# Twenty shared 4 KB places in SBUF, and the second layer's first attentions issued during the first pass

## Chip, cores and metric

One core of a Trainium2 chip runs the kernel as one program. The metric is the device time of one execution in microseconds (us), lower is better. Engines are named as in the profile: PE (TensorE, matrix products), PEld (its weight loads), DVE (VectorE), ACT (ScalarE), POOL (GpSimd) and SP (SyncE, which here only issues DMAs).

## The reference, cut to what matters

Two layers run over `x` of shape (8, 512, 256) in float32, with a context of 64 tokens of 192 per batch. Each block is added to the residual stream and sees a normalized `x`.

```python
# layer 0: cross attention (8 heads of 64), then top-4 of 16 experts of size 64
x = x + _L0_xattn_ref(_layernorm(x), ctx_768, mask_BxS2_bk0, ...)
x = x + _L0_ffn_ref(_layernorm(x), ...)
# layer 1: this block, with 4 heads of 32 and top-32 of 64 keys per head
def _L1_xattn_ref(x_text, x_vision, ...):
    scores = einsum("bthd,bghd->bhtg", Q, K) / sqrt(DH)
    topv, topi = top_k(scores, 32)
    attn = zeros_like(scores).at[bi, hi, ti, topi].set(softmax(topv))
    c_t = einsum("btg,bgd->btd", attn.mean(axis=1), V)
    x = layernorm(x_text) * (1 + gate * scale_in(c_t)) + gate * shift_in(c_t)
    y = s4d(x, log_dt, A, C, D_skip)          # a long convolution over 512 tokens
    y = y * (1 + gate * scale_out(c_t)) + gate * shift_out(c_t)
    xt = x_text + y
    xt = xt + gelu(layernorm(xt) @ W1 + b1) @ W2 + b2
    return layernorm(xt)
x = x + _L1_xattn_ref(_layernorm(x), ...)
# layer 1: 8 experts, each takes the 512 tokens (of 4096) with its highest scores
x = x + _L1_ffn_ref(_layernorm(x), ...)
```

## The kernel before, in words

**Tiling.** The 4096 tokens are 8 batches of 512 (B, S), each four tiles of 128 tokens on the partitions (TPB). A batch of `x` is a tile of 128 x 1024 float32, that is 4 KB on each partition.

**Stages.** A *first pass* runs layer 0 for each batch b: `attend0(b)` (scores against `M0`, a softmax on DVE, POOL and ACT, values through `VO`), `route0(b)` (the gates; `wd` goes to DRAM and comes back spread over the partitions as `wB`), and `experts0(b)` (`xT` x `keys` into PSUM, then L754 on DVE turns the product into `wB`, then `wB` x `vals` on PE, and the result is stored to `mid_x`). Beside it, `conv_kernel` (`build`) makes the spectrum `Kf` of the long convolution in small DVE operations. A *second pass* runs most of layer 1: `attend1(b)` loads `xb` from `mid_x`, makes the scores (L902), runs the top-k of 32 in four rounds of MAX8 (L938) and MATCH_REPLACE (L939) per head and tile, then the weights (L919 to L928), transposes them and makes the filmed input `xi`; `convolve(b)` is the transform (`FX`), the product with `Kf` (L993, L1001) and the way back (`IW`), filmed again (`Fout`); `dense1(b)` is the two-layer GELU block (`hT`,`w` and `w`,`gT` matmuls); `settle(b)` and `offer(b)` normalize, score for the last experts and store `out` and `tab`. Then `ending` loads what the last experts need; a threshold search in 13 rounds finds each expert's 512 tokens; and the last stage runs the 8 experts (`listed`, `yT`, `fc1`, `gT`, `fc2`), gathering rows from `tab` and adding rows to `out` by indirect DMAs.

**What sets the order.** Both passes are Python generators, one per batch and stage, and each `yield` ends a step. A list `parts` (from L1212 on) holds (generator, number of steps, first due time, last due time); `emit` sorts all steps by due time and runs them in that order. A due time is in units of about one batch of the first pass and is written by hand. The tile framework then fixes each engine's instruction order and all waits before the run, from the order given, the dependencies and its own costs; on the chip each engine runs its list in order. `T2` = 7.967 is the due time at which the second pass starts, and batch b's second pass is shifted by `T2 + b`: its attention from `t + 0.047` to `t + 0.9`, its convolution to `t + 1.94`, `dense1` from `t + 2.25`. The experts of the first pass are due from b+1.6 to b+2.5.

**Where the data lie.** Tiles come from pools, and pools from two stacks, left and right. `M0` and `VO` (8 x 4 KB each), `xT`, the first pass's work tiles and those of `conv_kernel` lie on the left stack `sl`; `xa` (4 buffers), `keys`, `vals` and the routing's tiles on the right stack `sr`. `convolving` (due at T2) closes `sl` and only then allocates the pools of the second pass: `xb` (5 buffers), `xi` (3), the constants `wq1`, `mb1`, `tm`, `am`, the film weights, `FX`, and the work tiles of attention (`uT`, `qT`, `ex`, `sc1` with 5 buffers, `wrk1` with 4) and convolution (`t0` with 3, `t1` with 2). `dense` (due at 9.394) closes `sr` and allocates `IW`, `w1`, `w2` and the tiles of `dense1`, `settle` and `offer` (`hn`, `z`, `zT`). `ending` (due at T2 + 9.3) closes the second pass's left pools and allocates `fc_w` (two 8 KB buffers for each of the two weight matrices) for the last experts.

**Queues.** Nearly all loads and stores are issued by SP in program order: `xT`, `x`, `wd`, `wB`, `mid_x`, `xb`, `out`, `tab`, `fc`. A DMA that waits for its data or its buffer holds those behind it.

## Time and profile before

| | |
|---|---|
| time, median of 3 runs | 1293.17 us (1293.06 to 1298.84) |
| profiled execution, its own time | 1295.33 us |
| its span | 1293.6 us |
| mean granted PE clock | 0.942 |
| last matmul of the first pass (`wB` x `vals`) ends | about 505 us |
| first matmul of `dense1` (`hT` x `w`) | about 566 us |
| top-k (L938, L939) of batch 0, 1, 2, 3 runs in | 470 to 501, 518 to 553, 575 to 604, 633 to 664 us |
| threshold search | about 988 to 1016 us |
| matmuls of the last experts | 1036 to 1282 us |

How to read the profile: the page gives each engine's busy time over the span, then 40 slices of about 32 us in which a digit is the busy share in tenths (`PEclk` is the granted PE clock in tenths). A row of a stretch reads: from and to, length, then for each engine the busy us and the number of instructions, then the granted clock, the DMA share and GB/s. A row of a group reads: line, engine, operation, output and inputs, shapes, count, then busy us and mean ns, then idle time before it and what ended that. A row in order of time reads: start, length, engine, line, operation, and in brackets the idle time before it with what ended it. Matmuls are pipelined, so a matmul's recorded length is longer than its distance to the next one.

### The profile page before, as it was taken

What the parts mean: (1) busy time and instruction counts of PE and PEld (TensorE: products, weight loads), DVE (VectorE), ACT (ScalarE), POOL (GpSimd) and SP (SyncE); (2) the same over time, 40 slices, a digit from 0 to 9 for tenths busy, and PEclk for the clock granted to TensorE, in tenths of its full rate; (3) what the DMA queues carried; (4) which work ended last, traced back from release to release, by engine and by line L of the source; (5) the groups of instructions that cost most, each with busy time, mean ns of one, the idle gap of its engine ahead of it and who ended that gap; (6) DMA issues with size and microseconds to landing.
All of it is one profiled execution on the core that took longest, in us unless ns stands there. A gap on an engine that the chain in (4) does not pass through costs nothing. (4 is left out here: it accounts for less than half of the span.)

```text
span 1293.6 us, 16870 instructions
## 1 busy us (share of the span) xinstructions
PE 1140.8 (88%) x5468; PEld 719.7 (56%) x5468; DVE 791.0 (61%) x3334; ACT 395.9 (31%) x783; POOL 568.5 (44%) x800
## 2 busy tenths in 40 slices
PE   7998989888999979578899999998994299999995
PEld 3555656565666545245465565655673157666663
DVE  4479847748586468959799898988354602221110
ACT  2344121131313211032454555445343031222220
POOL 2333314323332212545678777777773114233331
PEclk9998999899999989789999999999997589999998
DMA  8003304303213423000010100000051014443321
GB/s 247 17 27 83 99 12 105 99 18 99 51 49 88 149 66 106 13 1 1 1 49 1 50 19 32 34 1 34 17 189 67 17 54 104 108 123 100 98 38 16
DMA packets 60749, 80.29 MB, mean 62 GB/s; under 512 B 6003, under 2 KB 45172, under 8 KB 60534
## 3 DMA queue, kind: packets, MB, share of 16 engines
q1 hardware_dynamic: 53254, 69.26, 18.0%
q0 software_dynamic: 6240, 8.79, 4.1%
q10 hardware_dynamic: 1168, 1.18, 0.3%
q8 instruction: 43, 0.70, 0.2%
q14 instruction: 44, 0.36, 0.1%
HBM read 62.04 MB, written 17.17 MB: 61 GB/s over the span
## 5 line engine op out<-in xcount | busy, mean ns | idle before, releaser
L259 PE MATMUL ps_o<-vals,wB 128*128 128x256 f32 x512 | 131.9, 404 | 21.5 <-DVE wB L754 21.4
L259 PEld LDWEIGHTS ps_o<-vals,wB 128*128 128x128 f32 x512 | 100.4, 202 | 54.7 <-DVE wB L754 29.9
L198 PE MATMUL ps_m<-hT,w 128*128 128x512 f32 (+1 forms) x288 | 125.3, 560 | 0.1
L259 PE MATMUL ps_o<-w,gT 128*128 128x256 f32 x512 | 122.6, 380 | 1.1 <-ACT gT L1055 1.1
L198 PE MATMUL ps_m<-xT,keys 128*128 128x512 f32 x256 | 122.8, 605 | 0.0
L1403 POOL DMA_INDIRECT out<-o,idx x32 | 52.0, 1626 | 154.7 <-DVE o L1402 89.7
L198 PE MATMUL ps_m<-yT,fc 128*128 128x512 f32 x256 | 116.9, 606 | 0.8 <-issue 0.8
L1401 DVE TENSOR_TENSOR o<-ps_o,bb 128x256 f32<-128x256 f32 x32 | 13.6, 425 | 166.1 <-PE ps_o L198 163.5
L198 PE MATMUL ps_o<-fc,gT 128*128 128x256 f32 x512 | 114.7, 379 | 0.1
L259 PEld LDWEIGHTS ps_o<-w,gT 128*128 128x128 f32 x512 | 95.4, 190 | 30.2 <-issue 14.9
L198 PEld LDWEIGHTS ps_o<-fc,gT 128*128 128x128 f32 x512 | 96.5, 190 | 19.7 <-issue 7.2
L656 POOL TENSOR_TENSOR sc<-sc,mx 128x512 f32<-128x512 f32 x32 | 34.3, 1079 | 123.5 <-DVE mx L655 73.6
L1396 ACT ACTIVATE gT<-ps_m,bb 128x512 f32<-128x512 f32 x64 | 44.0, 688 | 127.2 <-PE ps_m L198 127.2
L198 PEld LDWEIGHTS ps_m<-yT,fc 128*128 128x128 f32 x256 | 49.2, 195 | 54.2 <-issue 53.4
L939 DVE MATCH_REPLACE8 wrk<-top,wrk 128x64 f32<-128x64 f32 x384 | 78.0, 212 | 0.0
L754 DVE SCALAR_TENSOR_TENSOR wB<-ps_m,wB 128x512 f32<-128x512 f32 x64 | 43.1, 678 | 53.2 <-DMA wB<-wd 27.3
L1001 POOL TENSOR_TENSOR t<-t,t 128x768 f32<-128x768 f32 x32 | 58.4, 1847 | 38.6 <-DVE t L993 33.0
L198 PEld LDWEIGHTS ps_m<-hT,w 128*128 128x128 f32 x288 | 53.3, 194 | 37.4 <-issue 33.1
L1055 ACT ACTIVATE gT<-ps_m,b 128x512 f32<-128x512 f32 (+1 forms) x72 | 45.3, 634 | 85.4 <-PE ps_m L198 81.8
L198 PEld LDWEIGHTS ps_m<-xT,keys 128*128 128x128 f32 x256 | 48.5, 195 | 39.9 <-issue 36.0
L938 DVE MAX8 top<-wrk 128x8 f32<-128x64 f32 x384 | 65.6, 214 | 0.0
L198 PE MATMUL ps_m<-VO,eT 128*128 128x256 f32 x256 | 61.5, 383 | 3.9 <-ACT eT L670 2.6
(356 smaller groups left out, 2224.2 us busy)
## 6 DMA issues: line engine op xcount, KB each, us to landing
wB<-wd SPq DMA_DIRECT2D x64, 256.0 KB, 4.9
fc<-in_fc1T SPq DMA_DIRECT2D x8, 1024.0 KB, 4.9
fc<-in_fc2T SPq DMA_DIRECT2D x8, 1024.0 KB, 5.6
xT<-in_xT SPq DMA_DIRECT2D x8, 512.0 KB, 7.0
xa<-in_x SPq DMA_DIRECT2D x8, 512.0 KB, 7.9
mid_x<-xa SPq DMA_DIRECT2D x8, 512.0 KB, 3.0
xb<-mid_x SPq DMA_DIRECT2D x8, 512.0 KB, 5.6
tab<-zt SPq DMA_DIRECT2D x7, 528.0 KB, 3.0
```

What stands on the lines that cost most here:

```text
L198: nc.tensor.matmul(ps, lhsT, rhs, start=(i == 0), stop=(i == n - 1))
L259: nc.tensor.matmul(acc[j // 2][:, (j % 2) * D : (j % 2 + 1) * D], h[:, j * P : (j + 1) * P], rhs[:, f, :], start=(f == 0 and j % 2 == 0), ...
L656: nc.gpsimd.tensor_tensor(sc, sc, bcast(mx.unsqueeze(2), [P, H0, SC]), ALU.subtract)
L754: nc.vector.scalar_tensor_tensor(wB, ps, 0.0, wB, ALU.max, ALU.mult)
L938: nc.vector.max(m8, src[:, h, :])
L939: nc.vector.match_replace(wrk[:, h, :], m8, src[:, h, :], -FMAX)
L1001: nc.gpsimd.tensor_tensor(ts[0][:, i], ts[0][:, i], ts[1][:, i], op)
L1055: nc.scalar.activation(g, ps, AF.Gelu, bias=ns.b1[:, f : f + 1])
L1396: nc.scalar.activation(gT[:, f, :], ps, AF.Gelu_apprx_tanh, bias=ns.bb1[:, c : c + 1])
L1401: nc.vector.tensor_tensor(o, pso[:, :D], ns.bb2[:, e, :], ALU.add)
L1403: nc.gpsimd.indirect_dma_start(out=out, out_offset=bass.IndirectOffsetOnAxis(ap=idx[:, q : q + 1], axis=0), in_=o, in_offset=None, compute ...
```

## The change

One tile `places` of 20 x 4 KB per partition is allocated at the start and kept to the end, and a table says which tile lies in which place. `M0` and `VO` are views of places 0 to 15, `xa` takes 16 to 19, and the tiles of the second pass and of the last experts take the places of earlier users. What the second attention needs (`wq1`, `mb1`, `tm`, the two `am`, `qT`, `kblk`) is allocated at the start too, and a new part `for_second` prepares it. `film("in", b)` is called after the top-k instead of before it. `IW` is loaded in `convolving`. `k_t` in `conv_kernel` has half its size. The due times are new: `T2` is 6.886, the attentions of batches 0, 1 and 2 have due times of their own (5.5, 7.184, 8.7), and so have their convolutions (8.1, 8.66, 9.952).

```diff
+    am_of = [eb.tile([P, TPB, P], F32, name="am%d" % i) for i in range(2)]
...
+    aq = pool(ctx, "a1_q")
+    places = pool(ctx, "places").tile([P, 2 * B + TPB, TPB * D], F32, name="places")
+    PLACES = {
+        "xa": (16, 17, 18, 19),
+        "xb": (3, 10, 4, 11, 12, 19),
+        "xi": (13, 14, 15, 0),
+        "sc1": (1,),
+        "ex": (2,),
+        "uT": (8,),
+        "wrk1": (9,),
+        "hn": (16,),
+        "z": (17,),
+        "zT": (18,),
+        "Kt": (0,),
+        "yT": (3, 10),
+    }
+    def place(name, b):
+        own = PLACES[name]
+        return places[:, own[b % len(own)]].rearrange("p (j d) -> p j d", d=D)
...
-    xa = pool(sr, "xa", 4, side="right")
...
-        xs[b] = xa.tile([P, TPB, D], F32, name="xa")
+        xs[b] = place("xa", b)
...
-    M0 = cw.tile([P, 2, B, H0, SC], F32, name="M0")
-    VO = cw.tile([P, B, H0 // 2, D], F32, name="VO")
+    M0 = places[:, 0:B].rearrange("p b (k h j) -> p k b h j", k=2, h=H0)
+    VO = places[:, B : 2 * B].rearrange("p b (q d) -> p b q d", d=D)
...
+    m8 = load(aq, "mb1_u8", a["mask2"].partition_broadcast(P), [P, B * SC], U8, nc.scalar)
+    tm8 = load(aq, "tm8", a["tmask"], [P, NTILE], U8, nc.scalar)
...
+    def for_second():
+        nc.sync.dma_start(wq1, a["Wq1"].rearrange("(k p) n -> p k n", p=P))
+        yield
+        yield from centered(wq1, P, 1)
+        nc.vector.tensor_scalar(wq1, wq1, 1.0 / math.sqrt(32.0), None, ALU.mult)
+        nc.vector.tensor_scalar(mb1, m8, 1.0, FMAX, ALU.subtract, ALU.mult)
+        nc.vector.tensor_scalar(tm, tm8, 1.0 / H1, None, ALU.mult)
...
-                t = kts[0].tile([P, 2, nd, 16], F32, name="k_t")[:, :, :, :m]
+                t = kts[0].tile([P, nd, 16], F32, name="k_t")[:, :, :m]
                 tt(X[:, :, :, m : 2 * m], X[:, :, :, 0:m], zr, ALU.mult)
                 yield
-                for g in range(2):
-                    tt(t[:, g], X[:, 1 - g, :, 0:m], zi, ALU.mult)
+                for g, op in enumerate((ALU.subtract, ALU.add)):
+                    tt(t, X[:, 1 - g, :, 0:m], zi, ALU.mult)
                     yield
-                for g, op in enumerate((ALU.subtract, ALU.add)):
-                    tt(X[:, g, :, m : 2 * m], X[:, g, :, m : 2 * m], t[:, g], op)
+                    tt(X[:, g, :, m : 2 * m], X[:, g, :, m : 2 * m], t, op)
                     yield
...
-        ns.xb_p = pool(ctx, "xb", 5)
-        ns.xi_p = pool(ctx, "xi", 3)
...
+        ns.IW = load(a1c, "IW", a["IW"].rearrange("(f p) t -> p f t", p=P), [P, 4, P])
...
-        xb = xbs[b] = ns.xb_p.tile([P, TPB, D], F32, name="xb")
+        xb = xbs[b] = place("xb", b)
...
-            sc = ns.a1t.tile([P, H1, SC], F32, name="sc1", bufs=5)
+            sc = by_head(place("sc1", b))[:, j]
...
+        if b % 2 == 0:
+            film("in", b)
+        yield
         pa = ps_t(0)
...
-            ts = [ns.cvt.tile([P, 2, 3, D], F32, name="t%d" % c, bufs=3 - c) for c in range(2)]
+            ts = [
+                places[:, 5:8].rearrange("p s (n d) -> p (s n) d", d=D)[:, 6 * f : 6 * f + 6].rearrange(
+                    "p (u o) d -> p u o d", u=2
+                ),
+                ns.cvt.tile([P, 2, 3, D], F32, name="t1", bufs=2),
+            ]
...
-        f1 = ns.wpool.tile([P, 2, FF], F32, name="fc1")
+        f1 = places[:, 1:3] if e % 2 else places[:, 11:13]
...
-        f2 = ns.wpool.tile([P, NF, D], F32, name="fc2")
+        f2 = (places[:, 8:10] if e % 2 else places[:, 13:15]).rearrange("p s (c d) -> p (s c) d", d=D)
...
-    T2 = 7.967
+    T2 = 6.886
...
+        (for_second(), 3, 1.5, 3.0),
         (build, PARAM_STEPS, 1.17, 1.9),
-        (build, BUILD_STEPS - PARAM_STEPS, 1.9, 7.811),
+        (build, BUILD_STEPS - PARAM_STEPS, 1.9, 7.661),
...
-            (attend0(b), 10, b + 0.0, b + 1.0),
-            (route[b], 2, b + 1.0, b + 1.06),
-            (route[b], 2, b + 1.369, b + 1.555),
-            (experts0(b), 17, b + 1.6 + -0.05 * max(b - 5, 0), b + 2.5 + -0.05 * max(b - 5, 0)),
+            (attend0(b), 10, b + -0.111, b + 1.0),
+            (route[b], 2, b + 1.025, b + 1.04),
+            (route[b], 2, b + 1.135, b + 1.601),
+            (experts0(b), 17, b + 1.936 + -0.015 * max(b - 5, 0), b + 2.436 + -0.015 * max(b - 5, 0)),
...
-    parts += [(once(convolving), 1, T2, T2), (once(dense), 1, B + 1.394, B + 1.394)]
+    parts += [(once(convolving), 1, 8.01, 8.01), (once(dense), 1, B + 1.52, B + 1.52)]
+    early = (5.5, 7.184, 8.7)
     for b in range(B):
         t = T2 + b
+        u = early[b] if b < 3 else t
+        v = (8.1, 8.66, 9.952)[b] if b < 3 else t + 1
+        n = 0.5 if b < 3 else 1.0
         parts += [
-            (attends[b], 2, t + 0.047, t + 0.157),
-            (attends[b], 8, t + 0.145, t + 0.192),
-            (attends[b], 8, t + 0.192, t + 0.9),
...
-            (convs[b], 1, t + 1.071, t + 1.071),
-            (convs[b], 4, t + 1.2, t + 1.369),
...
+            (attends[b], 2, u + -0.02, u + 0.182),
+            (attends[b], 8, u + 0.249, u + 0.681),
+            (attends[b], 8, u + 0.681, u + 0.938),
...
+            (convs[b], 1, v + 0.035, v + 0.035),
+            (convs[b], 4, v + 0.224 * n, v + 0.5 * n),
...
-                (denses[b], 1, t + 2.25, t + 2.25),
-                (denses[b], 17, t + 2.28, t + 3.184),
-                (settle(b), 5, t + 3.131, t + 3.468),
...
+                (denses[b], 1, t + 2.7, t + 2.7),
+                (denses[b], 17, t + 2.718, t + 3.6),
+                (settle(b), 5, t + 3.628, t + 3.815),
...
-                u = t + 1.951 + 0.46 * h
+                u = t + 2.46 + 0.61 * h
...
-    parts.append((once(ending), 1, T2 + B + 1.3, T2 + B + 1.3))
+    parts.append((once(ending), 1, T2 + B + 1.946, T2 + B + 1.946))
...
-        yT = wk2.tile([P, 2, CAP], F32, name="yT")
+        yT = place("yT", e).rearrange("p (k j) d -> p k (j d)", k=2)
...
-        gT = wk2.tile([P, NF, CAP], F32, name="gT2")
+        gT = (places[:, 4:8] if e % 2 else places[:, 16:20]).rearrange("p s (f n) -> p (s f) n", n=CAP)
```

## The prediction

> **What bounds the kernel now.** I read the page first: busy shares, then the 40 slices.
>
> ```profile
> span 1293.6 us, 16870 instructions
> PE 1140.8 (88%) x5468; PEld 719.7 (56%) x5468; DVE 791.0 (61%) x3334; ACT 395.9 (31%) x783; POOL 568.5 (44%) x800
> ...
> PE   7998989888999979578899999998994299999995
> ...
> DVE  4479847748586468959799898988354602221110
> ...
> PEclk9998999899999989789999999999997589999998
> ```
>
> PE is the bound, but not everywhere: it sags in slices 14 to 19 (about 450 to 650 us) and in 30 and 31 (the threshold search), and the granted clock sags with it. DVE has slack in the first pass (283.6 of 425 us below) and stands mostly at 8 or 9 tenths from slice 15 to 27. So I took the busy time by stage, each cut where a first or last matmul of a kind stands: 505 us is the last matmul of the first pass (`vals`), 566 the first of `dense1` (`hT,w`), 985 about where the search begins.
>
> ```profile
> core 0: us, PE busy (x) PEld busy (x) DVE busy (x) ACT busy (x) POOL busy (x), PEclk, DMA share, GB/s
> 25.00:450.00 425.00, 392.60 (x2573) 250.09 (x2572) 283.60 (x824) 111.14 (x279) 139.33 (x217) 0.97 0.25 69
> 450.00:505.00 55.00, 46.20 (x157) 29.53 (x156) 41.35 (x258) 10.20 (x20) 10.21 (x21) 0.91 0.22 55
> 505.00:566.00 61.00, 38.84 (x93) 18.12 (x92) 49.62 (x267) 11.62 (x21) 34.50 (x47) 0.78 0.17 54
> 566.00:650.00 84.00, 74.86 (x241) 44.06 (x240) 65.36 (x378) 30.81 (x49) 43.18 (x56) 0.96 0.00 1
> 650.00:900.00 250.00, 236.08 (x907) 143.65 (x905) 228.69 (x1237) 125.77 (x230) 184.19 (x265) 1.00 0.09 29
> 900.00:985.00 85.00, 78.03 (x338) 54.33 (x337) 34.75 (x112) 39.28 (x86) 63.23 (x97) 0.95 0.28 94
> 985.00:1050.00 65.00, 27.52 (x137) 15.23 (x137) 33.24 (x144) 10.61 (x18) 12.50 (x18) 0.56 0.10 30
> ```
>
> The weak stretch is 505 to 566: 22 us of idle PE in 61, at a clock of 0.78. The order of time of PE there says why:
>
> ```profile
> 526.80 1.19 PE L198 MATMUL ps_m<-t,IW 128*128 128x256 f32 x2 [1.34 <-POOL t L1001]
> 529.61 2.05 PE L198 MATMUL ps_m<-F0Fout,amT 128*128 128x512 f32 x2 [1.62 <-DVE top L938]
> 533.26 2.93 PE L198 MATMUL ps_m<-t,IW 128*128 128x256 f32 x6 [1.60 <-POOL t L1001]
> 539.76 1.59 PE L198 MATMUL ps_m<-F0Fout,amT 128*128 128x512 f32 x2 [3.57 <-DVE top L938]
> ```
>
> The first pass is over, no `dense1` matmul is ready, and the convolution of batch 0 waits behind DVE's top-k (L938) of batch 1. This stretch is a matter of order; the work exists.
>
> **The change, term by term** (us, on the profiled span).
>
> *Gap between the passes.* In due times the last step of `experts0(7)` goes from 9.40 to 9.41 and the first step of `dense1(0)` from 10.217 to 9.586: the distance shrinks from 0.817 to 0.18 units. The 61 us of 505 to 566 make 75 us a unit there, so 0.18 is 13 us: **-48**. Ends: -38 (a gap of 23 us) to -61 (no gap).
>
> *What is moved in front.* The first attention of the second layer is now due at 5.5, 7.18 and 8.7 and the convolutions 0 and 1 at 8.1 and 8.66. So the PE work of 505 to 566 comes earlier (38.8 us busy at 0.78 of the clock, some 30 at full clock), and with it the attention of batch 2 and the convolution of batch 1, which ran after 566. I price these by the starts of matmuls in the order of time, 0.43 us apart for 512 columns, 0.215 for 256 and 0.11 for a transpose: attention 4 x 0.43 + 8 x 0.215 + 8 x 0.11 = 4.3, convolution 8 x 0.43 (`FX`) + 16 x 0.215 (`IW`) + 8 x 0.43 (`Fout`) = 10.3. Together 45 us, of which 12 stay in the remaining gap: 33 us are to be placed between 25 and 505. The cover is PE's idle time there, 32.4 + 8.8 = 41 us. At the share that the second pass reaches (236.08/250 = 0.944) 25 to 505 would take (392.6 + 46.2 + 33)/0.944 = 500 us instead of 480, +20; at the first pass's own share (0.924) 511, +31. I take **+25**; with no cover it is +33.
>
> DVE is the other cover. The costliest groups of one batch's attention there, over all eight batches:
>
> ```profile
> L939 DVE MATCH_REPLACE8 wrk<-top,wrk 128x64 f32<-128x64 f32 x384 | 78.0, 212 | 0.0
> L938 DVE MAX8 top<-wrk 128x8 f32<-128x64 f32 x384 | 65.6, 214 | 0.0
> ```
>
> and in the order of time on DVE:
>
> ```profile
> 480.93 0.60 DVE L938 MAX8 top<-wrk 128x8 f32<-128x64 f32 x4
> 481.44 0.07 DVE L939 MATCH_VALUE_LOAD wrk<-top,wrk 128x8 f32 x1
> 481.50 0.21 DVE L939 MATCH_REPLACE8 wrk<-top,wrk 128x64 f32<-128x64 f32 x1
> 481.63 0.08 DVE L939 MATCH_VALUE_LOAD wrk<-top,wrk 128x8 f32 x1
> ```
>
> The means of 0.21 us overlap: four MAX8 start within 0.51 us, and load and replace of one head are 0.127 apart from the next, so the 64 heads and rounds take 64 x 0.255 = 16 us. L902, L919, L921, L922 and L928 add (15.0 + 12.4 + 11.8 + 4.1 + 18.3)/8 = 8. That is 24 us a batch, and 72 for three; with some 36 for two convolutions' DVE part DVE would be at (283.6 + 41.4 + 108)/505 = 0.86 through the first pass, below the 0.91 (228.69/250) at which it runs beside a PE of 0.944. That the two mix is seen already: from 477 to 505 DVE was busy 27.3 of 28 us with this top-k, and PE 27.2 with `experts0(7)`. On POOL the attention is L941, L925, L924 and L883, (20.0 + 19.1 + 6.0 + 4.9)/8 = 6.3 us a batch, 19 for three, beside 139 busy of 425; on ACT its exponentials and copies are under 4 us a batch, beside 111 of 425.
>
> *The tail.* Six stretches of 54 us from 566 on hold one batch each; 900 to 985 holds the two batches with no attention beside them, 42.5 us each. With three attentions gone, batch 5 joins these: 54 - 42.5 = **-11**. Ends: 0 to -16 (the 14.6 us of PE work that left, at 0.92).
>
> *Experts later and denser.* `experts0(b)` moves from b+1.6..2.5 to b+1.936..2.436, its routing weights stay near b+1.1..1.6. The loads of `wB` so get a lead; DVE waited 27.3 us for them (L754, "DMA wB<-wd"), and PE 21.4 behind it, 13.9 of it between 25 and 450. That idle time is already spent as cover above, so 0, end -14. At the start `experts0(0)` is 0.34 units later, at some 55 us a unit up to +18 of idle PE if nothing else were ready; PE was busy 45.4 of 50 us between 75 and 125 with other ready work in its list. I take **+2**, nearer to the row that shows PE fed.
>
> *Shared places and DMAs.* Each place's earlier user is due well before the next one: `xb(0)` takes the place of `M0`'s batch 3, last read near 4.0, at 5.5; `t0` has two halves instead of three buffers, with 20 us and more between its users. `sc1` loses its fifth buffer: its L902 now waits for L941 on POOL (0.62 us) of the batch before, which ended some 20 us earlier in the windows of the second pass; behind it on DVE stands everything, `wB` included, so 0 with that cover and 0.6 us an event without it. `xb(5)` waits for the store of `xa(7)`, two units before; behind it on SP's queue stand only stores and later loads. Three loads of `xb` (512 KB, 5.6 us to landing), `wq1` and small rows move ahead on SP, past `wB` loads; the DMA share there is 0.25. `k_t` at half size makes L417's products alternate with their sums on one in-order engine, and the count stays. Two ACT queue loads come forward to the start. All this: **0**, end +5.
>
> *A rule that speaks against it.* The Trainium skill, "SBUF — State Buffer", section "Who interferes with whom": a DVE instruction with two SBUF inputs and a GpSimd instruction that reads SBUF exclude each other for the whole instruction. The trace does not show that price: POOL's 128x256 addition at L1040 has a median of 728 ns where DVE is 91% busy (566 to 900) and 726 where it is 41% (900 to 985). By the rule each of the 12 two-input L919 in three batches could hold POOL 0.42 us, an estimate of 5 us on an engine that is a third busy; by the row nothing.
>
> **Sum:** -48 + 25 - 11 + 2 = **-32**. The profiled execution took 1295.33 us around its span of 1293.6; the median shown is 1293.17. From the median: **1261 us**.
>
> **Rivals.**
>
> *No net gain.* The first pass grows by all that is put into it (+33), the gap stays at 23 us (-38), the tail gives nothing: -5, 1288, with 5 for DMAs 1293. For it: PE's idle pieces in the first pass are all under 4 us, so they take work in only if it is ready at that moment. Against: 477 to 505 us.
>
> *More.* The gap closes (-61), the work fits at 0.944 (+20), the tail gives 16: 1236. For it: `wB` in time, and no half clock between the passes. Against: PE never held 0.944 in the first pass.
>
> *Slower: DVE's order.* An experts step is 3.44 us of PE (two times 1.72 in the order of time) and one `wB` eviction of 0.68 on DVE, so DVE has 2.8 us to spare; a round of four heads is 1.02. Where three rounds stand ahead of an eviction, PE stalls. The attentions of batches 0 to 2 lie beside four batches' experts, 32 steps. An average stall of 1.0 us a step eats the gain; at 1.4 it is +45, **1306**. For it: PE's largest wait in the first pass is already this one (L259 on DVE wB). Against: the same 28 us.
>
> *It doesn't do what it says.* If the one tile of 20 places were tracked whole, every user would wait for every other, and the time would rise by hundreds of us. Against: `M0`, `scores` and `Kf` are single tiles used in parts, without such waits.
>
> **Chances.** Forecast (1240 to 1284) 0.60, more 0.10, none 0.13, slower by DVE's order 0.15, whole-tile waits 0.02. Within 0.5% (1286.7 to 1299.6) is about what a measurement of this kernel cannot tell from no change; I split "none" into 0.03 faster, 0.07 same, 0.03 slower. So faster 0.73, same 0.07, slower 0.20. The best ends give -48 + 20 - 16 - 14 = -58 (1235), the worst -38 + 33 + 18 = +13 (1306); 1237 to 1303 leaves out some 0.05 below and 0.12 above.
>
> **What would show it.** Right: top-k (L938) running before 450 us; the first `dense1` matmul less than 25 us after the last `vals` matmul; that last one at 525 to 540; the clock between the passes over 0.9; three batches at 43 us each before the search, which starts near 953. Wrong: last `vals` matmul after 560; PE waiting on DVE wB for over 50 us; a search at 985 or later; new waits that name places' users.

## The result: 6 us faster, and the profile after

The median fell from 1295.73 us (14 runs) to 1290.12 us (14 runs, 1286.31 to 1291.75): ratio 0.9954, 95% interval 0.9941 to 0.9967. Forecast were 1261 us and -32; the direction held, the size did not. The profiled execution has a span of 1286.4 us against 1293.6 before. First the page of after, the same lines as before:

```profile
span 1286.4 us, 16948 instructions
...
PE 1134.3 (88%) x5468; PEld 716.0 (56%) x5468; DVE 795.0 (62%) x3334; ACT 395.4 (31%) x781; POOL 568.4 (44%) x800
...
PE   7998989979899979998779999898974299999995
...
DVE  4459957847997884697987889795434602211110
...
PEclk9998989989899989999899999999997599999998
```

The sag of PE and of its clock between the passes is gone: slices 16 to 18 (counted from 0, 515 to 611 us) read 9, 9, 8, and the two digits 7 that follow (611 to 675 us) lie inside the second pass. Next the busy time by stage, cut at the same events: the last `vals` matmul is at 529 us (505 before), the first `hT,w` matmul of `dense1` at 542 (566 before), the search at 985 (991 before). The second fence is the kernel before from its first `dense1` matmul to its search, with the same columns.

```profile
core 0: us, PE busy (x) PEld busy (x) DVE busy (x) ACT busy (x) POOL busy (x), PEclk, DMA share, GB/s
25.00:450.00 425.00, 387.16 (x2546) 246.99 (x2547) 318.84 (x1144) 114.61 (x287) 143.49 (x225) 0.96 0.24 65
450.00:505.00 55.00, 48.52 (x177) 29.24 (x176) 38.30 (x151) 12.99 (x24) 16.19 (x22) 0.94 0.32 83
505.00:529.00 24.00, 24.00 (x89) 16.61 (x88) 10.97 (x29) 1.84 (x4) 6.30 (x5) 1.00 0.09 22
529.00:542.00 13.00, 10.97 (x32) 4.20 (x31) 10.42 (x23) 5.46 (x10) 8.93 (x15) 1.00 0.77 234
542.00:985.00 443.00, 394.18 (x1478) 241.10 (x1477) 330.10 (x1737) 197.05 (x366) 301.29 (x441) 0.97 0.11 35
```

```profile
566.00:991.00 425.00, 392.04 (x1495) 243.45 (x1494) 330.67 (x1733) 198.89 (x373) 294.66 (x426) 0.98 0.11 36
```

The gap of 61 us is 13 us at a clock of 1.00, as forecast. Up to the first `dense1` matmul the kernel is 24 us ahead. From there to the search it needs 443 us instead of 425 **for the same busy time** (PE 394.18 against 392.04, DVE 330.10 against 330.67), so 18 of the 24 us are lost there, 16 of them as idle time on PE. The lead shrinks at both ends of the stage. From the first `dense1` matmul to that of batch 2 the kernel after needs 136 us and the kernel before 123 (the same columns, after first):

```profile
542.00:678.00 136.00, 116.70 (x386) 67.44 (x385) 119.36 (x700) 50.20 (x83) 90.01 (x122) 0.95 0.03 7
```

```profile
566.00:689.00 123.00, 110.59 (x385) 66.16 (x384) 99.78 (x545) 51.80 (x87) 72.89 (x100) 0.97 0.05 14
```

PE is idle 19 us of this stretch instead of 12, while DVE does 20 us more: its top-k of batch 4 runs at 650 to 687 us, in front of the `dense1` of batch 2, and in the kernel before at 687 to 717. From there to the first `dense1` matmul of batch 6 both need the same (217 and 216 us), and from that one to the search 90 and 86 us. What follows the search takes some 302 us in both. The order of time on PE where the gap was (start, duration, what, in brackets the idle time before it and what ended it):

```profile
525.77 3.19 PE L259 MATMUL ps_o<-vals,wB 128*128 128x256 f32 x14
528.79 1.88 PE L198 MATMUL ps_m<-F0Fout,amT 128*128 128x512 f32 x4
530.87 1.96 PE L198 MATMUL ps_m<-F1Fin,amT 128*128 128x512 f32 x4 [0.20 <-DVE nm_a L161]
...
535.30 1.95 PE L198 MATMUL ps_m<-places,wq 128*128 128x512 f32 x4
...
541.60 0.66 PE L189 MATMUL ps_t<-ident,places 128*128 128x128 f32 x4 [1.41 <-ACT hT L1082]
542.09 1.88 PE L198 MATMUL ps_m<-hT,w 128*128 128x512 f32 x4
543.81 0.59 PE L198 MATMUL ps_m<-kblk,qT 128*128 128x256 f32 x2
```

The waits are at most 1.41 us. But `places,wq` at 535 and `kblk,qT` at 544 are the attention of batch 2: it was to be done by then, and it only begins. On DVE its top-k runs at 545 to 569 us; those of batches 0 and 1 at 322 to 357 and 424 to 460. In the kernel before they run at 469 to 499, 517 to 551 and, batch 2, 575 to 600. **At the first `dense1` matmul both kernels have two attentions behind them.** So the stage that follows holds the same work in both, as its busy time says.

### The profile page after: what moved, and what is told of

It is laid out like the page before. It is cut to its first block, busy times and chain, and to the rows that moved or that the text cites. A ratio compares the mean times of both kernels' runs of the same rounds, so it can differ in the third digit from the quotient of the medians.

```text
span 1286.4 us, 16948 instructions
## 1 busy us (share of the span) xinstructions
PE 1134.3 (88%) x5468; PEld 716.0 (56%) x5468; DVE 795.0 (62%) x3334; ACT 395.4 (31%) x781; POOL 568.4 (44%) x800
## 5 line engine op out<-in xcount | busy, mean ns | idle before, releaser
L259 PE MATMUL ps_o<-vals,wB 128*128 128x256 f32 x512 | 126.2, 391 | 10.8 <-DVE wB L801 10.7
L198 PE MATMUL ps_m<-places 128*128 128x512 f32 (+1 forms) x288 | 123.6, 604 | 0.7 <-ACT places L1430 0.7
L198 PE MATMUL ps_o<-places 128*128 128x256 f32 x512 | 114.7, 379 | 0.1
L198 PEld LDWEIGHTS ps_o<-places 128*128 128x128 f32 x512 | 96.5, 190 | 19.7 <-issue 7.2
L970 DVE MATCH_REPLACE8 places<-top,places 128x64 f32<-128x64 f32 x512 | 101.0, 203 | 0.0
L154 DVE BATCH_NORM_STATS2 bnst<-places 128x6 f32<-128x256 f32 x192 | 72.9, 414 | 20.9 <-POOL places L1117 12.8
L198 PEld LDWEIGHTS ps_m<-places 128*128 128x128 f32 (+1 forms) x288 | 51.4, 193 | 58.5 <-issue 52.6
L1441 ACT ACTIVATE places<-ps_m,bb 128x512 f32<-128x512 f32 x64 | 44.0, 687 | 126.7 <-PE ps_m L198 126.7
L969 DVE MAX8 top<-places 128x8 f32<-128x64 f32 x512 | 79.1, 206 | 0.1
L1040 POOL TENSOR_TENSOR places<-places,t 128x768 f32<-128x768 f32 x32 | 57.5, 1820 | 48.6 <-DVE t L1032 48.6
L189 PE MATMUL ps_t<-ident,places 128*128 128x128 f32 x256 | 49.0, 287 | 27.0 <-DVE places L720 7.9
```

The costliest lines, as they stand in the source:

```text
L154: nc.vector.bn_stats(st, src)
L189: nc.tensor.transpose(ps[:, j * P : (j + 1) * P], r[:, k * P : (k + 1) * P], ident)
L198: nc.tensor.matmul(ps, lhsT, rhs, start=(i == 0), stop=(i == n - 1))
L259: nc.tensor.matmul(acc[j // 2][:, (j % 2) * D : (j % 2 + 1) * D], h[:, j * P : (j + 1) * P], rhs[:, f, :], start=(f == 0 and j % 2 == 0), ...
L969: nc.vector.max(m8, src[:, h, :])
L970: nc.vector.match_replace(wrk[:, h, :], m8, src[:, h, :], -FMAX)
```

## The experiments

A table first, to read all of them by the same three cuts (us in the profiled execution): end of the first pass (last `vals` matmul), the gap from there to the first `dense1` matmul, the stage from that matmul to the search. The ratio is to the kernel before, timed on the same chip in turn, with its 95% interval.

| kernel | first pass ends | gap | stage | ratio |
|---|---|---|---|---|
| before | 505 | 61 | 425 | 1 |
| after | 529 | 13 | 443 | 0.9954 (0.9941 to 0.9967) |
| a_bnst8 | 533 | 14 | 451 | 1.0055 (1.0041 to 1.0069) |
| b_offers_later | 529 | 14 | 449 | 1.0011 (1.0000 to 1.0022) |
| c_attn2_early | 531 | 29 | 447 | 1.0121 (1.0106 to 1.0137) |
| d_before_bnst8 | 510 | 67 | 440 | 1.0152 (1.0138 to 1.0166) |
| e_places_old_due | 524 | 55 | 436 | 1.0180 (1.0166 to 1.0194) |
| f_none_early | 535 | 29 | 448 | 1.0159 (1.0145 to 1.0173) |
| g_conv2_first | 530 | 13 | 498 | 1.0389 (1.0364 to 1.0413) |
| h_before_shake | 507 | 60 | 424 | 1.0046 (1.0032 to 1.0060) |
| i_after_shake | 530 | 12 | 451 | 1.0055 (1.0037 to 1.0072) |
| j_no_move | 519 | 55 | 450 | 1.0246 (1.0230 to 1.0261) |
| k_dense_closer | 530 | 12 | 445 | 0.9978 (0.9969 to 0.9986) |
| l_before_first_dues | 506 | 70 | 427 | 1.0072 (1.0059 to 1.0085) |
| m_pad | 522 | 12 | 442 | 0.9892 (0.9875 to 0.9909) |
| n_no_move_pad | 509 | 54 | 453 | 1.0208 (1.0189 to 1.0226) |
| p_pad_dense_closer | 523 | 12 | 444 | 0.9925 (0.9908 to 0.9943) |
| r_before_slide | 517 | 60 | 424 | 1.0091 (1.0072 to 1.0111) |
| s_old_spacing | 522 | 13 | 464 | 1.0060 (1.0045 to 1.0076) |

### First theory: a queue cuts dense1(1)

In after, `dense1(1)` runs 20 of its 32 `hT,w` matmuls at 599 to 617 us and the other 12 only behind the matmuls of `offer(0)` at 659.7. Theory 1 said that this cut costs the time, theory 2 that too few attentions moved, theory 3 that the shared places make tiles wait. Four kernels:

```diff
 a_bnst8
-            st = small.tile([P, 6], F32, name="bnst")
+            st = small.tile([P, 6], F32, name="bnst", bufs=8)
 b_offers_later (both lines; batch 6 keeps its time)
-                (offers[b], 1, t + 4.1 - 0.25 * (b == B - 2), t + 4.1 - 0.25 * (b == B - 2)),
+                (offers[b], 1, t + 4.5 - 0.65 * (b == B - 2), t + 4.5 - 0.65 * (b == B - 2)),
 c_attn2_early
-    early = (5.5, 7.184, 8.7)
+    early = (5.5, 7.184, 7.95)
 e_places_old_due (and every other due time of the kernel before)
-    T2 = 6.886
+    T2 = 7.967
```

> The changed kernel with eight buffers instead of four for the small tile bnst (the statistics of one row tile, L153), nothing else. Theory 1 (queues): in the changed kernel the additions of dense1(0) are done on DVE at 577.9 to 579.1 us, but its mv_out aggregates run only at 641.9 to 643 us, because the four bnst buffers are handed out in program order and conv(2)'s statistics stand ahead while conv(2) itself waits behind the top-k of batch 3; so settle(0) and offer(0) come late, and dense1(1), of whose 32 hT,w matmuls 20 run at 599 to 617 us, stops until offer(0)'s matmuls at 659.7 us. With eight buffers the aggregates come before 620 us, dense1(1) loses less than 15 us in the middle, and the time falls by 10 to 18 us, to 1272 to 1280. Theory 2 (DVE as a whole bounds the second pass, because only two of eight attentions moved): the statistics move, but the time does not: within 4 us of the changed kernel. Theory 3 (waits on the shared places): within 4 us too, and dense1(1) still stops.

> The changed kernel with the due times of offer(0) to offer(5) 0.4 of a batch later (4.5 and 4.579 instead of 4.1 and 4.179), so that all of dense1(b+1) stands ahead of offer(b) on PE and in the two buffers of ps_m(1). Theory 1 (queues): dense1(1) is no longer cut at step 5 of 8: its 32 hT,w matmuls run without the stop from 617 to 660 us, the batch of dense work that is left over after the last offers gets 12 matmuls shorter (about 11 us of PE's time), and the kernel gets 6 to 12 us faster, to 1278 to 1284. Theory 2 (DVE bounds the second pass): the order on PE changes, the time does not, within 4 us. Theory 3: within 4 us.

> The changed kernel with the second attention of batch 2 due at 7.95 instead of 8.7, and nothing else. Its top-k runs at 545 to 569 us in the changed kernel, after the first pass, while those of batches 0 and 1 run at 322 to 357 and 424 to 459 us. Theory 2 (too little moved): the top-k of batch 2 comes before 530 us, DVE, which is busy 10 to 12 of 25 us from 475 to 525 us, takes it there for nothing, the second pass has 24 us of DVE less, and the kernel gets 8 to 15 us faster, to 1275 to 1282. Theory 1 (queues): the cut of dense1(1) stays, because it hangs on conv(2) and the statistics behind it; 0 to 5 us faster. Theory 3: 0.

> The storage of the changed kernel (twenty shared places, the constants of the second attention loaded early) with all due times of the kernel before: no second attention stands beside the first pass. Theories 1 and 2: the places cost nothing by themselves, so the time is that of the kernel before within 5 us (against the changed kernel: 2 to 10 us slower). Theory 3 (the shared places make tiles wait for one another): over 6 us slower than the kernel before, with waits of the loads into xa or xb or of the first writes of ex, wrk1, z and zT for the last reader of another tile.

None came out as theory 1 or 2 had it. b does what it says: the 32 matmuls run through, to 629 us. But `dense1(2)` starts at 678 us, as in after. Four stretches of 25 us show what became of the gap on PE, first of after, then of b (columns as above):

```profile
625.00:650.00 25.00, 16.86 (x44) 8.43 (x45) 19.12 (x71) 8.94 (x17) 16.56 (x29) 0.82 0.00 0
650.00:675.00 25.00, 21.23 (x86) 12.36 (x85) 25.00 (x167) 10.90 (x22) 22.14 (x27) 0.97 0.01 1
```

```profile
625.00:650.00 25.00, 21.48 (x73) 12.10 (x72) 19.00 (x64) 10.34 (x21) 15.78 (x27) 0.93 0.00 0
650.00:675.00 25.00, 15.20 (x53) 6.81 (x53) 25.00 (x157) 7.99 (x19) 22.70 (x29) 0.81 0.00 1
```

PE's hole moved from the first stretch to the second; DVE is busy 19 and 25 of 25 us in both kernels. Theory 1 falls: work that PE does earlier there is missing later. a still had the cut (`dense1(1)` to 672 us), so it tests less than it was meant to. In c the top-k of batch 2 did come early, at 490 to 529 us, and the stage from the first `dense1` matmul to the search did lose DVE work:

```profile
560.00:1007.00 447.00, 394.25 (x1457) 241.56 (x1456) 306.79 (x1520) 192.38 (x361) 287.92 (x420) 0.95 0.11 35
```

306.79 against 330.10 us of DVE, about the 24 us of one attention, and yet 447 us of stage; and with that top-k among the convolution of batch 0 on DVE (its products at 509 to 527, its `yv` at 534 to 543) the first `dense1` matmul went from 542 to 560. So theory 2 has no support either: in this order, with a third attention out of the stage, nothing is won. e was 24 us slower than before; the waits in it that name the earlier user of a place are small (loads of `xb` behind a store of the place, 5.1 us in two of them, on SP's queue alone). The storage seemed to cost 24 us, unless old due times on new storage are bad for another reason; further down 5 to 12 us of it are found, and the rest of e's 24 stays open.

### How much an edit without meaning costs

All engines' orders are made anew from every edit. So two kernels got an edit that changes no work: more buffers for `bnst` in the kernel before, and one due time shifted by 0.02 in both.

```diff
 d_before_bnst8
-            st = small.tile([P, 6], F32, name="bnst")
+            st = small.tile([P, 6], F32, name="bnst", bufs=8)
 h_before_shake, i_after_shake
-        (build, PARAM_STEPS, 1.17, 1.9),
+        (build, PARAM_STEPS, 1.17, 1.88),
```

> The kernel before with eight buffers instead of four for the small tile bnst, nothing else: the control of a_bnst8. The first four runs overturned theory 1 (the cut of dense1(1) went away in b_offers_later and the kernel got 5 us slower) and showed that three edits of the changed kernel that each do what they say (a_bnst8, b_offers_later, c_attn2_early) lose 5 to 20 us. Theory 4 (order): the orders of all five engines are made anew by every edit, the due times of a kernel were fitted to its own orders, and an edit that is worth nothing by itself loses some 5 to 20 us. Then this one, whose two orders differ in the same way, is 5 to 20 us slower than the kernel before. If instead the number of buffers had a cost or a gain of its own in the changed kernel alone, this one is within 4 us of the kernel before.

> The kernel before, in which the last of the first filter parameters are due at 1.88 instead of 1.9 of a batch, an edit that changes no work and no storage: a shake of the order. Theory 4 (order): 5 to 20 us slower than the kernel before, and the ends of the value matmuls of the eight batches move by several us against 144, 192, 241, 301, 356, 404, 461 and 505 us. Theory 3 (the shared places cost 24 us by themselves, as e_places_old_due would have it): the order is robust, within 4 us of the kernel before.

> The changed kernel with the last of the first filter parameters due at 1.88 instead of 1.9: the same shake that made the kernel before 5 us slower (h_before_shake), no work and no storage changed. Theory 4 (order): 0 to 20 us slower than the changed kernel's 1290. If the order is robust in the changed kernel: within 4 us.

The ratio moved by +1.52%, +0.46% and, against after, +1.01%: 6 to 20 us. The net result of the change, 6 us, is no larger than the smallest of these, so how much of it the change earns and how much this order is not shown. From here on I read totals only for effects above this and otherwise the end of a stage: the first pass is steadier, it ends at 505, 510, 507 and 506 us in the four kernels with the old storage and no move (before, d, h and l, which comes below), and at 529, 529, 530 and 533 in after, b, i and a. The stage behind it is not steady: the shakes alone move it from 425 to 440 (d) and from 443 to 451 (i).

### The move taken back

```diff
 f_none_early
-    early = (5.5, 7.184, 8.7)
+    early = (T2, T2 + 1, T2 + 2)
-        v = (8.1, 8.66, 9.952)[b] if b < 3 else t + 1
+        v = (8.1, 8.9, 9.952)[b] if b < 3 else t + 1
 j_no_move (early as in f, and)
+    T2 = 7.967
+        v = t + 1
+        n = 1.0
```

> The changed kernel with the second attentions of batches 0, 1 and 2 due as those of the others are, at 6.886, 7.886 and 8.886 instead of 5.5, 7.184 and 8.7 (conv(1) at 8.9 instead of 8.66, since it follows its attention); storage and all other due times stay. It takes back the move of the attentions alone. If the move is worth what the prediction gave it (48 us of gap less 25 us of work in front): the top-k of batch 0 comes after 420 us, that of batch 1 after 500 us, the first pass ends 10 to 20 us earlier than at 529 us, the gap in front of the first dense1 matmul grows from 13 to 40 us or more, and the kernel gets 15 to 30 us slower than the changed one, 1305 to 1320. If the gain of the changed kernel came from its other due times: within 8 us of the changed kernel.

> The changed kernel with the second pass due 1.081 of a batch later (T2 = 7.967 as in the kernel before) and no attention earlier than that: storage, the due times of the first pass and the spacing inside the second pass stay. The move itself is taken back whole. By the prediction's terms (gap of 48 us come back, 25 us of work in front gone, 11 us of tail gone, the other way round): the first pass ends at 505 to 515 us, the first dense1 matmul comes at 560 to 575 us, and the kernel is 25 to 40 us slower than the changed one, 1315 to 1330, that is slower than the kernel before, because the other due times were set for the move. If the move is worth little: within 10 us of 1290.

f takes back less than it was meant to: with T2 still 1.08 units earlier, the top-k of batch 0 runs from 387 us and that of batch 1 from 469, both still in the first pass, which ends at 535 us and not 10 to 20 us earlier than in after; the gap is 29 us, not 40. It loses 2% against after. j takes back all: the gap is 55 us again, the kernel 2.9% slower than after (1.0246 against 0.9954), 37 us, and slower than the kernel before, as expected. **With the rest of the change kept, the move is worth 37 us here and 41 us between n and m below**, more than any shake above and about the -34 of the three terms that the forecast had for it (-48, +25, -11). The rest of the change, without the move, costs 32 us against the kernel before; part of that can be the order, since no due time was fitted to this kernel. One thing did not fit: the first pass of j, with no more beside it than in the kernel before, ends at 519 us, not at 505 to 510.

### What lengthens the first pass: a slide

```diff
 l_before_first_dues (route, build and dense in the same way)
-            (attend0(b), 10, b + 0.0, b + 1.0),
+            (attend0(b), 10, b + -0.111, b + 1.0),
-            (experts0(b), 17, b + 1.6 + -0.05 * max(b - 5, 0), b + 2.5 + -0.05 * max(b - 5, 0)),
+            (experts0(b), 17, b + 1.936 + -0.015 * max(b - 5, 0), b + 2.436 + -0.015 * max(b - 5, 0)),
```

> The kernel before with the changed kernel's due times for the first pass alone (attend0, route, experts0, the filters' end at 7.661, dense at 9.52); storage and second pass stay. The first pass of the changed kernel ends 24 us later than before, but its first three batches, beside which no second attention ran, are late already by 5, 9 and 9 us. If the work moved in front sets the end of the first pass (the prediction): this one ends the first pass at 505 us give or take 5. If the due times of the first pass do: 512 to 520 us. The time of the whole lies 0 to 20 us above the kernel before by theory 4.

The first pass of l ends at 506 us: its due times are not it. So it is the storage (e: 524, j: 519). The DMA issues on SP's queue show a difference in every kernel with the places. Here, in order of time, a line of PE and a line of SP's queue of the kernel before, and then the same two of after:

```profile
71.83 1.25 PE L198 MATMUL ps_m<-wo,vT 64*64 64x256 f32 x10
```

```profile
73.15 1.20 SPq L448 DMA_DIRECT2D ldt<-in_log_dt  x2
```

```profile
84.59 1.98 PE L198 MATMUL ps_m<-ctxT,wv 96*128 96x512 f32 x4
```

```profile
86.66 1.20 SPq L496 DMA_DIRECT2D ldt<-in_log_dt  x2
```

Each load starts within 0.1 us of the end of a matmul that reads weights: before, the last `wo,vT` (71.83 + 1.25 = 73.08); after, the last `ctxT,wv` (84.59 + 1.98 = 86.57).

`ldt` and its neighbours are the parameters of the filter that `build` makes. After takes `Kt` (4 KB) and `dskip` (1 KB) out of the pool `kg`. The pool `kp` of the parameters lies behind it and slid down by 5 KB, as these two lines say from memory last read by the `wo,vT` matmuls onto memory last read by `ctxT,wv`, 13 us later. So the filter starts 13 us later, and its DVE work falls more into the time from 100 us on, where `wB` is due. To test it, 5 KB were put back in front of `kp` in three kernels, and in r the slide was made alone in the kernel before:

```diff
 m_pad (on after), n_no_move_pad (on j), p_pad_dense_closer (on k)
             with ExitStack() as sp:
+                pool(sp, "pad").tile([P, TPB * D + D], F32, name="pad")
                 yield from params_in(pool(sp, "kp"))
 r_before_slide (on the kernel before)
-        dskip = kg.tile([1, D], F32, name="dskip")
-        Kt = kg.tile([P, TPB, D], F32, name="Kt")
...
                 yield from seeds(pool(sp, "ks"))
+            kl = pool(stack, "kl")
+            dskip[0] = kl.tile([1, D], F32, name="dskip")
+            Kts[0] = kl.tile([P, TPB, D], F32, name="Kt")
```

> The changed kernel with an unused tile of 5 KB in front of the filter's parameter tiles (pool kp), which puts these back on the memory that they have in the kernel before; it is given back before the next pool opens. In all six kernels with the shared places so far that were looked at, the load of ldt is issued at 85.6 to 86.7 us, right behind the last ctxT,wv matmul, and in the four with the old storage at 73.2 to 74.7, right behind the last wo,vT matmul: with Kt (4 KB) and dskip (1 KB) taken out of the pool below, the parameter tiles slid onto weights that are still read. Theory 6 (slide): ldt is issued at 73 to 78 us, PE's waits for wB between 100 and 210 us fall, the second batch ends its value matmuls at 192 to 196 us instead of 201, the first pass ends 5 to 12 us before 529 us, and the kernel gets 3 to 12 us faster, to 1278 to 1287. Theory 4 (order): ldt comes early, but the time is not below the changed kernel's by more than 3 us.

> j_no_move (storage of the changed kernel, no attention moved) with the same 5 KB in front of the parameter tiles. j_no_move ends its first pass at 519 us, the kernels with the old storage at 505 to 510. Theory 6 (slide): 506 to 513 us, and 5 to 15 us faster than j_no_move's 1327. If other parts of the storage lengthen the first pass: still 516 us or later.

> The kernel before with Kt and dskip allocated behind the parameter tiles instead of in front of them: the slide alone, with the old storage. Theory 6: ldt is issued at 84 to 88 us instead of 73, the second batch ends its value matmuls 5 to 9 us after 192 us, the first pass ends at 510 to 520 us instead of 505, and the kernel is 5 to 25 us slower than before (the shake of the order, 5 and 19 us in h_before_shake and d_before_bnst8, is in it). If the late parameters cost nothing: the first pass ends within 3 us of 505 to 510 us.

m_pad loads `ldt` where the kernel before does (SP's queue in order of time):

```profile
73.26 1.20 SPq L497 DMA_DIRECT2D ldt<-in_log_dt  x2
```

and what PE waits for `wB` between 100 and 210 us (in total, times, longest) is, in the waits of before, of after and of m_pad in turn,

```profile
PE ps_o L259 <- DVE wB L754: 5.1, 6, 1.7
```

```profile
PE ps_o L259 <- DVE wB L801: 8.6, 3, 4.2
```

```profile
PE ps_o L259 <- DVE wB L802: 2.5, 1, 2.5
```

The second batch ends its value matmuls at 193 us (before 192, after 201), the first pass at 522 instead of 529, and in n at 509 instead of 519. r, with the slide alone, loads `ldt` at 86.4 us and ends the first pass at 517 instead of 505. In four pairs the ratio moves the same way: after to m -0.62%, j to n -0.38%, k to p -0.53%, before to r +0.91%, that is 5 to 12 us. Each alone is no more than a shake of the order, and the second batch is not a sure sign: r ends it at 196 us, short of the 5 to 9 us that were expected, and a, e and i, which load `ldt` late too, at 193 to 195. The third batch is: in the eight kernels of the table that load `ldt` at 73 to 75 us it ends its value matmuls at 241 to 245 us, and PE waits 2.5 to 6.0 us for `wB` between 100 and 210; in the eleven that load it at 86 to 87 us, at 249 to 255, with 7.5 to 12.0 us of waits. With that, and four pairs of one sign, the slide is shown. **m_pad is the fastest kernel of the study: 1279.3 us, 1.1% under the kernel before.**

### The second pass: not settled

```diff
 k_dense_closer (s in place of t for dense1, settle, offer and the tail)
+        s = t - 0.21 * min(b, 2)
 g_conv2_first
-        v = (8.1, 8.66, 9.952)[b] if b < 3 else t + 1
+        v = (8.1, 8.66, 9.7)[b] if b < 3 else t + 1
 s_old_spacing (on m_pad; all other due times of the second pass as before, but for batches 0 to 2)
-    T2 = 6.886
+    T2 = 7.336
```

> The changed kernel with dense1, settle and offer due 0.21 of a batch earlier for batch 1 and 0.42 earlier for batches 2 to 7, the spacing behind the attention that the kernel before has. In the changed kernel dense1(5) starts 99 us behind the end of the top-k of batch 5, in the kernel before 79 us; dense1(5) to dense1(6) takes 53 us although all top-k is done at 856. Theory 5 (the dense work was put half a batch further behind the attention, so what three early attentions gained is given back at the end): the distance falls to 75 to 85 us, the search begins before 975 us and the kernel is 10 to 20 us faster than the changed one, 1270 to 1280. Theory 4 (order): the distance falls, but holes appear elsewhere on PE; not faster by more than 4 us.

> The two edits of the changed kernel together that have a reason in the traces: the 5 KB in front of the parameter tiles and dense1, settle and offer closer behind the attention (k_dense_closer, 1291). If theory 6 holds and the order does not eat it: 1278 to 1287. By theory 4: 1288 to 1305.

> The changed kernel with the convolution of batch 2 due at 9.7 instead of 9.952, in front of the top-k of batch 3 on DVE instead of behind it. In the changed kernel DVE runs that top-k at 598 to 626 us, yv of conv(2) only at 627 to 640, PE waits for it (4.3 us at 628) and has 12.0 and 18.6 us of work in the two 25 us stretches from 625 to 675, and dense1(2) starts at 678 us. Theory 2a (top-k(3) in front of conv(2) makes the hole in PE's work): dense1(2) starts before 665 us, and the kernel is 5 to 15 us faster than the changed one. Theory 4 (order): dense1(2) starts earlier too, but the top-k of batches 3 to 7 come later by as much and the kernel is within 5 us of the changed one or slower.

> m_pad with the spacing of the kernel before inside the second pass (attention and convolution of batches 3 to 7, dense1, settle, offer and the tail, T2 = 7.336 so that dense1(0) stays due at 9.6); the three early attentions stay as they are. From the first dense1 matmul to the search the five profiled kernels with the old spacing take 424 to 440 us (425 in the kernel before), the kernels with the new one and no move 450 to 453, and with the move 442 to 447. Theory 7 (the move does save the forecast 7 to 11 us there, but the new spacing costs 17 to 25): about 415 to 430 us here, the search begins at 950 to 965 us instead of 976, and the kernel is 10 to 25 us faster than m_pad, 1254 to 1270. Theory 4 (order: the old spacing is only good with the old order): 440 us or more, not faster than m_pad.

k did bring `dense1(5)` from 99 to 80 us behind the top-k of its batch, and the stage stayed at 445 us; with the pad (p against m) it is 0.3% slower. g put the convolution first as meant, and PE's in-order queue stopped elsewhere: the transposes of `offer(0)` waited for POOL's part of `settle(0)`, and `dense1(1)` behind them. PE's waits in g have this line:

```profile
PE ps_t L189 <- POOL places L1117: 17.3, 2, 16.5
```

s was to bring the stage to 415 to 430 us and needed 464. Its stretches, columns as above:

```profile
600.00:625.00 25.00, 23.84 (x84) 15.41 (x83) 9.37 (x24) 6.08 (x11) 11.42 (x13) 1.00 0.01 2
625.00:650.00 25.00, 11.35 (x40) 4.65 (x38) 25.00 (x196) 13.63 (x27) 19.98 (x32) 0.66 0.00 0
675.00:700.00 25.00, 24.28 (x101) 15.37 (x100) 15.28 (x93) 8.30 (x17) 8.71 (x10) 1.00 0.15 43
700.00:725.00 25.00, 13.35 (x24) 6.68 (x24) 24.62 (x144) 2.99 (x5) 13.37 (x20) 0.59 0.06 22
```

PE runs through three batches of `dense1` by 695 us while DVE is left at 9 of 25 us, and then PE starves while DVE catches up. The two engines take turns where they should run side by side; a lead in attention is used up at once, not spread over the pass.

## Why the prediction was right in direction and wrong in size

- **Gap, -48: right.** 61 to 13 us, clock 1.00. In the kernels without the move it is 54 to 70 us.
- **What is moved in front, +25: the sum right by luck.** The first pass ends 24 us later. Where the slide is taken out, the moved work makes it 13 us longer (n 509, m 522), 4 us lie between before and n, which is within a shake, and 7 are the slide, which the forecast did not have. And less work came in front than the 33 us of PE and 108 us of DVE in the sum: by the rows of the stages, from 25 us to the end of the first pass PE is busy 459.68 us in after and 438.80 before, 21 more, and DVE 368.11 and 324.95, 43 more. The third attention is not in it.
- **Experts later, +2: right.** Their due times alone end the first pass at 506 (l), and in after PE waits 10.7 us for `wB` instead of 21.4.
- **Shared places and DMAs, 0, end +5: wrong.** I went through who shares a place with whom and found no wait, and none that costs much shows (in e 5.1 us on SP's queue). I did not ask what the tiles lie on that stayed in the pools from which others were taken out. Measured: 5 to 12 us, 8 in after.
- **The tail, -11, end 0 to -16: the step that failed.** It said "With three attentions gone, batch 5 joins these". After the first `dense1` matmul no attention had gone: two were done there before and after, the busy time of PE and of DVE is the same to 2.2 us, so there was nothing for batch 5 to join. `dense1(5)` to `dense1(6)` still takes 52 us (53 before). The stage took +18 instead, 16 of it idle time on PE; 13 of the 18 come before the `dense1` of batch 2, where DVE works ahead on attention. That is 29 us against the forecast; the span missed it by 25 (-7 instead of -32), since the first pass took 3 us less than forecast and the part behind the search 1 less. And in c, with the third attention really gone, the stage was no shorter (447 us), so the step did not hold there either.
- **A term that I left out, its size not shown: the new spacing of the second pass.** I priced what the change moves and not that it also sets all due times after it anew. Without the move the stage takes 450 and 453 us with the new spacing (j, n), 424 to 440 with the old one (before, d, e, h, l, r): 10 us apart at the least, and with the move 7 to 11 us less (j to after, n to m). But a shake alone moves this stage by 15 (d) and 8 us (i), so neither size is shown, and s says that the old spacing doesn't serve the moved kernel either. Why 443 us are needed for this work is open; moving single due times did not shorten it in b, c, g or k.
- **The rivals.** "No net gain", 1288 to 1293, holds the time, for other reasons than it gave: the gap did close, and the first pass grew by 24, not 33. "DVE's order" is refuted by the halved wait for `wB`. Tracking of the whole tile is refuted by n, whose eight ends of the value matmuls, batch by batch (144, 192, 241, 299, 355, 404, 472, 509) are within 4 us those of before (144, 192, 241, 301, 356, 404, 461, 505) but for the seventh.
- **The signs.** Top-k before 450 us: for two of three batches begun. Last `vals` at 525 to 540, gap under 25, clock over 0.9: all came. Three batches at 43 us, search near 953: did not, and "a search at 985 or later" was named as a sign of being wrong.
- **The rule on the port that DVE and GpSimd share: read from the wrong engine.** The Trainium skill, "SBUF — State Buffer", section "Who interferes with whom", says that the two exclude each other for a whole instruction. The prediction looked at POOL's durations and concluded that the trace shows no price, and on POOL there is hardly any: its 128x768 sum takes 1847 ns in the mean before (L1001) and 1820 after (L1040). But it shows on DVE. One line of POOL, then three of DVE, in order of time, from after:

```profile
111.14 2.09 POOL L708 TENSOR_TENSOR sc<-sc,sm 128x512 f32<-128x512 f32 x2 [0.93 <-DVE ldt L468]
```

```profile
111.26 1.07 DVE L476 SCALAR_TENSOR_TENSOR kp<-ldt,kp 128x128 f32<-128x128 f32 x1
112.25 1.12 DVE L476 SCALAR_TENSOR_TENSOR kp<-kp,kp 128x128 f32<-128x128 f32 x1
113.30 0.28 DVE L478 SCALAR_TENSOR_TENSOR kp<-ldt,kp 128x128 f32<-128x128 f32 x1
```

Beside POOL's two sums a DVE instruction with two inputs of 128x128 takes 1.07 and 1.12 us, and 0.28 right behind them: the rows agree with the page. The kernel before has the same (1.13 and 1.12 us at 110.75 and 111.79, beside POOL's sums). What this costs a whole kernel no run here tells; it stands in both kernels.

## What to carry to other kernels

A gain from moved work is priced in the stage that it leaves: ask what of it was already done when that stage began, and compare the busy time of the stage after, not only its length. Where tiles leave a pool that is laid out like a stack, everything above slides; look at what the first tiles behind now lie on, and when its last reader ends. Where every edit remakes the order, measure first what an edit without meaning costs, and read experiments by the end of a stage that stays steady under such edits rather than by totals.

## What the runs showed of the hardware that was not expected

Idle time on PE goes with a lower granted clock: in s the stretch with 11.35 us of PE in 25 has a clock of 0.66, the one with 13.35 us 0.59, and those with 24 us have 1.00; in after 16.86 us go with 0.82. Closing a gap may so gain more than its idle time: the same 5468 matmuls are busy 1140.8 us before and 1134.3 after; that the clock makes this difference is not shown. In what pieces the idle time comes may matter too: from 529 to 542 us in after the pieces are at most 1.41 us and the clock is 1.00, from 625 to 650 one is 4.29 us and it is 0.82; the busy shares differ as well (10.97 of 13 and 16.86 of 25), so this is not settled here. The Trainium skill, "TensorE: Matmul & The Clock Gate", section "Part 1: The HAM clock gate", says that the throttled clock is the default and that activity releases it; the rows of s and after agree.
